# Two chained SCNN layers (five-tap scans down, up, right and left): the last pair's output on two DMA queues with a sixth residual tile, one transfer for the identity, and the second input's statistics on ScalarE

## The chip, the cores and the metric

The kernel runs on one NeuronCore of a Trainium2 chip. The metric is the device time of one execution in microseconds (us). Matrix products run on TensorE (PE in the profile), element-wise work on VectorE (DVE), ScalarE (ACT) and GpSimd (POOL). DMAs are issued from two queues: SyncE's (SP) and ScalarE's (ACTq in a timeline; its transfers are counted as q10, those of SP as q1). A queue issues in order, and an ACT instruction that stands behind an ACT DMA issue waits for it.

## The reference

The input is x of shape (32, 48, 64, 128) in float32: 32 images, 48 channels, 64 rows, 128 columns. Two layers each do x = x + conv(groupnorm(x)), where `conv` is four scans in sequence. Each scan carries one line of the image and adds to the next line a five-tap convolution of it over channels and the other axis:

```python
def step(w, b):
    def f(carry, inp):
        nxt = inp + _conv1d(carry, w, b)      # 48x48 channels, 5 taps
        return (nxt, nxt)
    return f
...
_, d_rest = jax.lax.scan(step(down_w, down_b), d0, xs[1:])      # rows 1..63
...
_, u_rest = jax.lax.scan(step(down_w, down_b), u0, seq)         # rows 62..0, same weights
...
_, r_rest = jax.lax.scan(step(right_w, right_b), r0, ws[1:])    # columns 1..127
...
_, l_rest = jax.lax.scan(step(left_w, left_b), l0, R[Ww - 2::-1])
...
x = x + _L0_conv_ref(_gn(x), ...)
x = x + _L1_conv_ref(_gn(x), ...)
```

`_gn` is a group norm of 16 groups of 3 channels, with mean and variance over a whole image and no learned scale. A scan is serial: 63 steps down, 63 up, 127 right, 127 left.

## The kernel before, in words

**Tiling.** The 32 images are four groups of eight (g = 0 to 3), and two groups make a pair. A scan step is nine matmuls of 128x128 into three PSUM tiles, followed by three VectorE adds (line 660) that add bias and input, and the next step needs their result. A line of an image lies over 128 partitions in three pieces (`NG` = 3): eight interleaved positions (`e`) times 48 channels. The list `PIECES` says which channels of which position lie where, so a load or a store of one piece is three or four DMAs (`pieces(o)`: three for o = 0 and o = 2, four for o = 1).

**Phases.** `PHASES` lists twelve. A "rows" phase does the down and up scan of one group (126 steps), a "cols" phase the right and left scan of one pair (254 steps). The order is rows x0, rows x1, cols pair 0, rows x2, then those of layer 1 mixed in, and last cols (1,0) and cols (1,1). Layer 0's normalised input comes from `xin`, a permuted copy of x in DRAM; results of layer 0 go to `mid`; the up scan's result goes to `upa` or `upb` and is read back by columns.

**Memory.** One big tile, `arena`, holds three slots of 6 units each and four stage units (a unit is 128 partitions x 2048 floats, 1 MB). A pair in a cols phase has four quarters of the width; quarter j lies in slot j % 3, so quarters 0 and 3 share a slot: quarter 0 is written to `spill` after the right scan has passed it and read back (`spill_unit(..., True)`) after quarter 3 has been given out.

**Order.** There is no automatic scheduler. `at(t, fn, ...)` puts a call in an agenda at scan step t (counted over all phases), and each engine's and each queue's instructions are issued in that order. Times in the agenda are steps, of about 2 us each; the real waits come from data. The 8 DMA semaphores (they show as waits of the issuing instruction in the built program) are given out in turn over both queues, so a DMA waits until the one eight before it in program order has landed.

**The start.** `first_group` loads group 0 (`take`, two DMAs per image and half), makes an identity matrix in DRAM (`make_ident`: a block of zeros, then its first column of ones, each one DMA; read back with a row pitch one shorter, the ones fall on the diagonal) and reads it back into `to_row` in ten small DMAs mixed with the loads. The up to three DMAs held back per `let_go` follow between loads.

**The second input.** `plan_input(1, ...)` brings group 1 in during phase 0, in four blocks of 8 + 8 rows, t = 38, 51, 64, 77. Two block buffers (`nats1`) alternate. Of each block POOL makes four permuted tiles of two row pairs (`permute`, line 493, into two ring tiles) and SP writes them to `xin` (`put_out`). Statistics for images 0 to 3 come from VectorE (`stats.take`, line 340), those of 4 to 7 from ScalarE (`take_others`, lines 350 and 358: a pass for the sum and a pass for the squares). The block after next is loaded (`take_in`) at `free`, 12 steps after the block's t, and the fourth permuted tile is written at 12.25 steps. `scaling` then turns statistics into a scale and an offset, one stage per step, `move_rows` loads the rows of phase 1 from `xin`, and `scale_rows` (line 536) scales them on ScalarE before the scan uses them.

**The last pair.** In cols (1,1), each of 24 units (quarter 3 first, then 2, 1, 0) gets its residual (`load_residual`, on the ACT queue) into one of five tiles, an add (line 589: POOL; VectorE for quarter 0), a permute of eight copies over POOL and ACT (line 614; three engines for quarter 0) and its stores (`store_result`, all on SP, 128-byte runs in `out`). Units are planned 4.5 steps apart. The tile of unit u-2 is loaded again for unit u-2+5 after unit u. `last_loads` puts the residual loads of all six units of quarter 0 (20 DMAs) at one time, left + 97, and `last_results` does those six units after the last scan step. In cols (1,0) only quarter 3 is stored directly; the other three quarters are held in DRAM and let out in the next phase.

Of the kernel before, what the change touches and what calls it, by code (L numbers as in the profile page):

```python
# [33 lines left out]
C = 48  # L34
# [7 lines left out]
GB = 8  # L42
# [49 lines left out]
def kernel(  # L92
# [22 lines left out]
    NBN = H * W // (2 * BN)  # L115
    CHANNEL = H * W * GB
    PAD = 1024
    assert N == FULL and SLOT == NG * HALF * N and SLOT == 6 * UNIT

    cpool = ctx.enter_context(tc.tile_pool(name="cpool", bufs=1))  # L120
# [15 lines left out]
    arena = const([FULL, 3 * SLOT + 4 * UNIT], "arena")  # L136
    slot = [arena[:, i * SLOT : (i + 1) * SLOT] for i in range(3)]
    stage = arena[:, 3 * SLOT :].rearrange("p (i n) -> p i n", i=4)
    wt = {k: const([FULL, NG, NG * FULL], f"w{k}") for k in ("right", "left")}
    downs = const([FULL, 2, NG, NG * FULL], "downs")  # L140
    wt |= {f"down{i}": downs[:, i] for i in range(2)}
    spare_tile = downs.rearrange("p i g n -> p (i g n)")[:, 0:UNIT]
    bd = const([FULL, NG, 2, 3], "bd")
    mask_sb = const([P, P], "mask_sb")
    maskp = const([P, NG, FULL], "maskp")
    mask_in = const([FULL, NG, P], "mask_in")
    last = const([FULL, NG * N], "last")
    junk = const([FULL, BN], "junk")

    def kept(name):  # L150

# [470 lines left out]
    def store_result(k, j, i, perm):  # L622
        pair = PHASES[k][2]
        o, half = UNITS[i]
        for e, c0, c1, p0 in pieces(o):
            dst = in_output(j, 2 * pair + half, e)[c0 * NH : c1 * NH]
            src = perm[p0 : p0 + c1 - c0].rearrange("p (a b n) -> p a b n", a=NH, b=GB)
            dma(dst.rearrange("(c a) b n -> c a b n", a=NH), src)

    def hold_result(j, i, perm):  # L630
        o, half = UNITS[i]
# [110 lines left out]

    def plan_input(g, times, work, lag, nats, perms):

        stats = InputStats(f"x{g}", GB // 2 if g == 1 else 0)
        rows = nats[0].shape[-1] // W
        ahead, pieces_of = len(nats), rows * W // BN
        per = rows * W * GB // perms[0].shape[-1]
        for j, t in enumerate(times):
            nat = nats[j % ahead]  # L750
            if j == 0 and g > 1:
                at(t - 7, take_in, g, 0, nat)
            for i in range(per):
                perm, r = perms[i % len(perms)], i * rows // per
                at(t + i * work / per, permute, nat, r, perm, [nc.gpsimd])
                at(t + i * work / per + 4, put_out, g, 2 * rows * j + r, perm, rows)
            for b in range(stats.nv):
                at(t + lag + 1.25 * b, stats.take, pieces_of * j, nat, b)
            at(t + lag, stats.take_others, pieces_of * j, nat)
            if j + ahead < len(times):  # L760
                free = t + max(work, lag + 1.25 * stats.nv, 7)
                at(free, take_in, g, 2 * rows * (j + ahead), nat)
        spread(t + work + lag + (0, 0, 8, 5)[g], scaling(f"x{g}", 0, g, stats, x_masks), 1)

    def plan_rows(k, t0, prev):
        if k == 1:
# [33 lines left out]
    def plan_cols(k, t0, prev):  # L800
        _, layer, pair = PHASES[k]
        n = 2 * NG
        after = prev == "cols"
        for i in range(n):
            if follows(k) and UNITS[i][1] == 1:
                other = nc.scalar
                at(t0 - 31 + i, load_unit, k, 0, i, 4, NH, 0, E8, other)
                at(t0 - 13 + i, load_unit, k, 0, i, 2, 4, 0, E8, other)
                at(t0 - 6 + i / n, load_unit, k, 0, i, 1, 2, 0, E8, other)
                at(t0 - 1.5, load_unit, k, 0, i, 0, 1, E8 // 4, E8, other)  # L810
                at(t0, load_unit, k, 0, i, 0, 1, 0, E8 // 4, other)
            else:
                early = 30 if after else 46 if k == 2 else 70
                at(t0 - early + 2 * i, load_unit, k, 0, i)
            if follows(k):

                at(t0 + 1.5, load_unit, k, 1, i, 0, NH, 0, E8, nc.scalar)
            else:
                at(t0 + (3 if after else -24 + 2 * i), load_unit, k, 1, i)
            at(t0 + (38 if after else 8) + 2 * i, load_unit, k, 2, i)  # L820
            at(t0 + 33 + 2 * i, spill_unit, k, i, False)
            at(t0 + 50 + 2 * i, load_unit, k, 3, i)
        final = k == len(PHASES) - 1
        left = t0 + W - 1
        end = left + W - 1
        for i in range(n):
            at(left + 64 + 2 * i, spill_unit, k, i, True)
        units = []
        for n_done, j in enumerate((3, 2, 1, 0)):
            every = 4.5  # L830
            if j == 0 and PHASES[k + 1 if not final else k][0] == "rows":
                every = 7
            units += [(left + 34 + 32 * n_done + every * i, j, i) for i in range(n)]
        stats = None
        if layer == 0:
            stats = ResultStatsV(f"r{2 * pair}"), ResultStatsA(f"r{2 * pair + 1}")
        tiles = [stage[:, i] for i in range(4)]
        if layer:
            tiles.append(spare_tile)
        n = len(tiles)  # L840
        direct = [u for u in units if not (final and u[1] == 0)]

        for u, (t, j, i) in enumerate(direct):
            nat = tiles[u % n]
            o, half = UNITS[i]
            if u < n:
                at(left + 16, load_residual, k, j, i, nat)
            if layer == 0:
                if u >= n:
                    at(direct[u - n][0] + 3, load_residual, k, j, i, nat)  # L850
                at(t, add_residual, k, j, i, nat)
                at(t + 4, keep_result, k, j, i)
                unit = quarter(k, j)[:, half, o]
                if half == 0:
                    for b in range(GB):
                        at(t + 5 + b, stats[0].take, j, o, unit, b)
                else:
                    at(t + 1, stats[1].take, j, o, unit)
            else:

                at(t, add_residual, k, j, i, nat)
                at(t + 2.5, permute_unit, k, j, i, nat, (nc.gpsimd, nc.scalar, nc.scalar))
                if final or j not in HELD:
                    at(t + 4.5, store_result, k, j, i, nat)
                else:
                    at(t + 4.5, hold_result, j, i, nat)

                if u >= 2 and u - 2 + n < len(direct):
                    at(t + 4.6, load_residual, k, *direct[u - 2 + n][1:], tiles[(u - 2) % n])
        if layer == 0:  # L870
            t = units[-1][0] + 14
            g = 2 * pair
            spread(t, scaling(f"r{g}", 1, g, stats[0], r_masks), 1)
            spread(t + 20, scaling(f"r{g + 1}", 1, g + 1, stats[1], r_masks), 1)
        if layer:

            at(left + 10, nc.scalar.copy, junk[:, 0:1], quarter(k, 3)[:, 0, 0, RUN - 1 : RUN])
        if layer and not final:
            todo = [(j, half, e) for j in HELD for half in range(2) for e in range(E8)]
            for n, what in enumerate(todo):  # L880
                at(end + 63 + 1.9 * n, let_result, *what)
        if final:
            at(left + 97, last_loads, k)
            at(end + 4, last_results, k)

    def last_tiles(k):
# [1 line left out]
        s = slot[slots(k)[2]].rearrange("p (i n) -> p i n", i=2 * NG)  # L888
        return [s[:, i] for i in range(2 * NG)]

    def last_loads(k):
        for i, nat in enumerate(last_tiles(k)):
            load_residual(k, 0, i, nat)

    def last_results(k):

        for i, nat in enumerate(last_tiles(k)):
            perm = (*(stage[:, n] for n in range(4)), spare_tile)[i % 5]
            add_residual(k, 0, i, nat, nc.vector)
            permute_unit(k, 0, i, perm, (nc.scalar, nc.gpsimd, nc.vector))  # L900
            store_result(k, 0, i, perm)
# [10 lines left out]

    tiles = [stage[0:P, i] for i in range(4)]
    nats1 = [wide_nat(2 * SLOT + i * UNIT * 4, 8) for i in range(2)]
    plan_input(1, [starts[0] + 38 + 13 * j for j in range(4)], 11, 7, nats1, tiles[2:4])
    nats = [wide_nat(3 * SLOT, 4)]
    times = [starts[2] + 16 + 13.5 * j for j in range(8)]
    plan_input(2, times, 6, 6, nats, tiles[2:4])
# [13 lines left out]
    def first_group():  # L932
# [10 lines left out]
        spare = {k: wt[k].rearrange("p i n -> p (i n)") for k in ("down1", "right", "left")}  # L943
        to_row = [spare["right"][0:C, i * FULL : (i + 1) * FULL] for i in range(9)]
        to_row += [spare["left"][0:C, 0:FULL]]
        zero, one = last[0:C, 0 : C + 1], last[0:C, C + 1 : C + 2]
        ident = dram.tile([C, C + 1], F32, tag="ident", name="ident")
        square = ident.rearrange("c n -> (c n)")[0 : C * C].rearrange("(c n) -> c n", n=C)

        def make_ident():  # L950
            dma(ident, zero)
            dma(ident[:, 0:1], one)
            for m, (e, c0, c1, o, p0) in zip(to_row, PIECES):
                hold(m[c0:c1, p0 : p0 + c1 - c0], square[c0:c1, c0:c1])

        rows = HALF // 2
        parts = [wide_nat(SLOT + i * 2 * HALF * N * 2, rows) for i in range(2)]
        nc.vector.memset(zero, 0.0)
        nc.vector.memset(one, 1.0)
        for b in range(2 * GB):  # L960
            if b == 2:
                nc.vector.memset(spare["right"], 0.0)
# [37 lines left out]
                    ps.rearrange("p (r n) -> p r n", n=N),  # L1000
                )

        for b in range(3):
            take(0, b)
        make_ident()
        load_weights("down0", 0, DOWN, hold)
        load_constants(hold)
        for b in range(3, GB):
# [123 lines left out]
```

## Time and profile before

| what | us |
|---|---|
| median of 3 runs | 4410.18 (4403.57 to 4413.39) |
| the profiled execution | 4416.53 |
| its span | 4414.7 |
| PE busy | 4154.9 |
| first scan step starts | 149.25 |
| last scan step ends | 4311 |

The span is what the profile covers; 1.8 us lie outside. PE is busy nearly throughout, but that is no measure of a limit: matmuls wait for the previous step's adds. Between the first and the last step PE stands still for some 82 us, 33 of them before 500 us. DMA share is the mean busy share of 16 DMA engines; it goes over 1.00 where transfers of both queues overlap. PEclk is the granted clock.

### The profile page before, as it was taken

The page shows a single profiled execution, that of the slowest core. Times are in us where ns is not written, and L with a number is a line of the kernel's source. Part 1 is how long each engine was busy: PE and PEld are TensorE (multiplying, and loading weights), DVE is VectorE, ACT ScalarE, POOL GpSimd, SP SyncE. Part 2 cuts the span into 40 slices and gives each one's busy share as a digit, 9 for nine tenths or more (in the row PEclk, how much of TensorE's full clock was granted, in tenths as well). Part 3 has the DMA queues.
Part 4 walks back from the last instruction along what each step waited for, and adds up shares of the span by engine and source line. Part 5 has one row for each costly group of instructions (what it writes and reads, how often), then busy time and mean ns, then how long its engine had stood idle before and what let it go on. Part 6 is the DMA issues. An engine that isn't in the chain of part 4 may idle for free.

```text
span 4414.7 us, 89966 instructions
## 1 busy us (share of the span) xinstructions
PE 4154.9 (94%) x36632; PEld 4125.1 (93%) x36632; DVE 2183.1 (49%) x6594; ACT 1311.1 (30%) x2570; POOL 829.0 (19%) x775
## 2 busy tenths in 40 slices
PE   4889998999999999998999999999999999999990
PEld 1889998999999999998999999999999999999990
DVE  5454443446664444443446665444444444444442
ACT  1743301434794545100006764403000011110112
POOL 4342000324332020000004410000000034410443
PEclk9999999999999999999999999999999999999995
DMA  9988879865998989579407989849187059999799
GB/s 180 178 164 152 129 139 186 223 123 186 234 196 147 156 157 160 92 124 207 72 1 238 226 166 139 119 67 163 30 147 169 1 105 229 251 239 162 137 220 148
DMA packets 2111230, 680.34 MB, mean 154 GB/s; under 512 B 2000992, under 2 KB 2053984, under 8 KB 2070880
## 3 DMA queue, kind: packets, MB, share of 16 engines
q1 hardware_dynamic: 2092992, 586.49, 70.0%
q10 hardware_dynamic: 17824, 88.10, 8.4%
q8 instruction: 288, 4.72, 0.5%
q14 instruction: 126, 1.03, 0.1%
HBM read 397.57 MB, written 295.98 MB: 157 GB/s over the span
## 4 chain that ended last, share of the span: by engine, by line
PE 85%; DMA 6%; ACT 4%; SPq 3%; issue 1%; POOL 1%; DVE 0%; ACTq 0%; POOLq 0%; DVEq 0%
PE step_01r L651 6%; PE step_00r L651 6%; PE step_10r L651 6%; PE step_00l L651 6%; PE step_10l L651 6%; PE step_01l L651 6%; PE step_11l L651 5%; PE step_11r L651 4%; PE step_11d L651 3%; PE step_10u L651 3%; PE step_11u L651 3%; PE step_12d L651 3%; PE step_13u L651 3%; PE step_12u L651 3%; PE step_13d L651 3%; PE step_03d L651 3%
## 5 line engine op out<-in xcount | busy, mean ns | idle before, releaser
L536 ACT ACTIVATE arena<-arena,offset,scale 128x256 f32<-128x256 f32 (+2 forms) x864 | 600.9, 790 | 404.0 <-DVE arena L660 214.5
L589 POOL TENSOR_TENSOR arena<-arena 128x2048 f32<-128x2048 f32 x83 | 376.3, 4549 | 1722.3 <-PE step_01l L651 533.4
L493 POOL COPY arena<-arena 112x256 f32<-112x256 f32 x458 | 271.0, 649 | 753.4 <-DMA arena<-in_x 522.7
L427 ACT ACTIVATE junk<-arena 128x256 f32<-128x256 f32 x192 | 129.6, 675 | 693.3 <-DMA arena<-xin 553.2
L651 PE MATMUL step_00r<-arena,wright 128*128 128x128 f32 x2286 | 257.7, 276 | 21.1 <-DMA arena<-upa 21.1
L651 PE MATMUL step_01r<-arena,wright 128*128 128x128 f32 x2286 | 258.0, 277 | 20.8 <-DMA arena<-upa 20.8
L651 PEld LDWEIGHTS step_00r<-arena,wright 128*128 128x128 f32 x2286 | 257.5, 193 | 21.3 <-issue 21.2
L651 PEld LDWEIGHTS step_01r<-arena,wright 128*128 128x128 f32 x2286 | 257.8, 193 | 21.0 <-issue 20.9
L651 PE MATMUL step_11r<-arena,wright 128*128 128x128 f32 x2286 | 258.8, 277 | 5.1 <-DVE arena L660 5.1
L651 PEld LDWEIGHTS step_11r<-arena,wright 128*128 128x128 f32 x2286 | 258.3, 193 | 5.5 <-DVE arena L660 5.3
L651 PE MATMUL step_00l<-arena,wleft 128*128 128x128 f32 x2286 | 256.3, 275 | 0.0
L651 PE MATMUL step_10r<-arena,wright 128*128 128x128 f32 x2286 | 256.1, 275 | 0.0
L651 PEld LDWEIGHTS step_10r<-arena,wright 128*128 128x128 f32 x2286 | 255.8, 192 | 0.3
L651 PEld LDWEIGHTS step_00l<-arena,wleft 128*128 128x128 f32 x2286 | 255.7, 192 | 0.0
L651 PE MATMUL step_11l<-arena,wleft 128*128 128x128 f32 x2286 | 255.5, 275 | 0.0
L651 PE MATMUL step_10l<-arena,wleft 128*128 128x128 f32 x2286 | 255.5, 275 | 0.0
L651 PE MATMUL step_01l<-arena,wleft 128*128 128x128 f32 x2286 | 255.4, 275 | 0.0
L651 PEld LDWEIGHTS step_11l<-arena,wleft 128*128 128x128 f32 x2286 | 255.4, 192 | 0.0
L651 PEld LDWEIGHTS step_10l<-arena,wleft 128*128 128x128 f32 x2286 | 255.4, 192 | 0.0
L651 PEld LDWEIGHTS step_01l<-arena,wleft 128*128 128x128 f32 x2286 | 255.3, 192 | 0.0
L614 ACT COPY arena<-arena 128x256 f32<-128x256 f32 x190 | 109.6, 655 | 474.4 <-POOL arena L589 246.9
L358 ACT ACTIVATE junk<-arena 112x512 f32<-112x512 f32 x160 | 101.0, 631 | 501.3 <-DMA arena<-in_x 253.9
(177 smaller groups left out, 7025.9 us busy)
## 6 DMA issues: line engine op xcount, KB each, us to landing
xin<-arena SPq DMA_DIRECT2D x96, 384.0 KB, 5.4
arena<-xin SPq DMA_DIRECT2D x96, 384.0 KB, 8.2
mid<-arena SPq DMA_DIRECT2D x96, 384.0 KB, 7.8
arena<-mid SPq DMA_DIRECT2D x192, 192.0 KB, 4.3
upb<-arena SPq DMA_DIRECT2D x192, 192.0 KB, 3.9
arena<-upb SPq DMA_DIRECT2D x96, 384.0 KB, 11.4
arena<-xin SPq DMA_DIRECT2D x186, 192.0 KB, 4.3
upa<-arena SPq DMA_DIRECT2D x180, 192.0 KB, 3.9
```

What stands on the lines that cost most here:

```text
L358: nc.scalar.activation(junk[0:P], piece, AF.Identity, accum_out=self.sum[:, at[0], at[1]],)
L427: nc.scalar.activation(junk[:, 0:n], view[:, b], AF.Identity, accum_out=self.sum[:, i, j : j + 1])
L493: copy(dst[:, r, q], src[:, r0 + r, q])
L536: nc.scalar.activation(args[0], args[0], AF.Identity, bias=args[2], scale=args[1])
L589: eng.tensor_tensor(unit, unit, nat, ALU.add)
L614: copy(by_w(perm)[:, a], src[:, a])
L651: nc.tensor.matmul(part(whole(ps[o]), -s), weights[:, i, FULL * (o - NG * s - i + 1) : FULL * (o - NG * s - i + 2)], part(src(i), s), star ...
```

## The change

- Identity: the block of zeros and the ones are set together in SBUF and written to DRAM in one DMA, after the first image's loads and not after the third's.
- Second input: all eight images' statistics go to ScalarE, from step t + 2 (before t + 7); a block buffer is loaded again at t + 13.5 for g = 1 (before t + 12), which lies behind the write of the fourth permuted tile; `scaling` starts at step 93 (before 95).
- Layer 1's two cols phases: `spill` is read back a unit at a time from left + 39.5, 4.5 steps apart, each behind the unit's stores (before: from left + 64, 2 apart).
- Last pair: every second store goes to the ACT queue; a sixth residual tile; the residual of a unit of quarter 0 is loaded behind the same unit of quarter 1 and `last_loads` is gone; quarter 0's six permuted units have six tiles (before five).
- To make room, two weights, `last` and `junk` lie with `down0` and `down1` in one tile, `early`, of which two units are used as residual tiles at the end.

```diff
-    downs = const([FULL, 2, NG, NG * FULL], "downs")
-    spare_tile = downs.rearrange("p i g n -> p (i g n)")[:, 0:UNIT]
+    early = const([FULL, 3 * WEIGHTS + NG * N + BN], "early")
+    spare_tiles = [early[:, i * UNIT : (i + 1) * UNIT] for i in range(2)]
...
     def store_result(k, j, i, perm):
-        for e, c0, c1, p0 in pieces(o):
+        for n, (e, c0, c1, p0) in enumerate(pieces(o)):
...
-            dma(dst.rearrange("(c a) b n -> c a b n", a=NH), src)
+            queue = nc.scalar if n % 2 and k == len(PHASES) - 1 else nc.sync
+            dma(dst.rearrange("(c a) b n -> c a b n", a=NH), src, queue)
...
-        stats = InputStats(f"x{g}", GB // 2 if g == 1 else 0)
+        stats = InputStats(f"x{g}", 0)
...
-            for b in range(stats.nv):
-                at(t + lag + 1.25 * b, stats.take, pieces_of * j, nat, b)
             at(t + lag, stats.take_others, pieces_of * j, nat)
             if j + ahead < len(times):
-                free = t + max(work, lag + 1.25 * stats.nv, 7)
+                free = t + (13.5 if g == 1 else 7)
                 at(free, take_in, g, 2 * rows * (j + ahead), nat)
-        spread(t + work + lag + (0, 0, 8, 5)[g], scaling(f"x{g}", 0, g, stats, x_masks), 1)
+        spread(t + work + lag + (0, 3, 8, 5)[g], scaling(f"x{g}", 0, g, stats, x_masks), 1)
...
-            at(left + 64 + 2 * i, spill_unit, k, i, True)
+            t = left + 64 + 2 * i if layer == 0 else left + 39.5 + 4.5 * i
+            at(t, spill_unit, k, i, True)
...
-            tiles.append(spare_tile)
+            tiles += spare_tiles[0 : 2 if final else 1]
...
+                if final and j == 1:
+                    at(t + 4.7, load_residual, k, 0, i, last_tiles(k)[i])
...
-            at(left + 97, last_loads, k)
...
-            perm = (*(stage[:, n] for n in range(4)), spare_tile)[i % 5]
+            perm = (*(stage[:, n] for n in range(4)), *spare_tiles)[i]
...
-    plan_input(1, [starts[0] + 38 + 13 * j for j in range(4)], 11, 7, nats1, tiles[2:4])
+    plan_input(1, [starts[0] + 38 + 13 * j for j in range(4)], 11, 2, nats1, tiles[2:4])
...
         def make_ident():
-            dma(ident, zero)
-            dma(ident[:, 0:1], one)
+            dma(ident, one)
...
-        nc.vector.memset(zero, 0.0)
-        nc.vector.memset(one, 1.0)
+        nc.vector.memset(one, 0.0)
+        nc.vector.memset(one[:, 0:1], 1.0)
...
-        for b in range(3):
+        take(0, 0)
+        make_ident()
+        for b in range(1, 3):
             take(0, b)
-        make_ident()
```

More of the change, by code (lines that the diff above doesn't have):

```diff
@@ L117 @@
     PAD = 1024
+    WEIGHTS = NG * NG * FULL
     assert N == FULL and SLOT == NG * HALF * N and SLOT == 6 * UNIT
@@ L138 @@
     stage = arena[:, 3 * SLOT :].rearrange("p (i n) -> p i n", i=4)
-    wt = {k: const([FULL, NG, NG * FULL], f"w{k}") for k in ("right", "left")}
-    downs = const([FULL, 2, NG, NG * FULL], "downs")
-    wt |= {f"down{i}": downs[:, i] for i in range(2)}
-    spare_tile = downs.rearrange("p i g n -> p (i g n)")[:, 0:UNIT]
+    early = const([FULL, 3 * WEIGHTS + NG * N + BN], "early")
+    spare_tiles = [early[:, i * UNIT : (i + 1) * UNIT] for i in range(2)]
+    wt = {
+        k: early[:, i * WEIGHTS : (i + 1) * WEIGHTS].rearrange("p (i n) -> p i n", i=NG)
+        for i, k in enumerate(("down0", "down1", "right"))
+    }
+    wt["left"] = const([FULL, NG, NG * FULL], "wleft")
     bd = const([FULL, NG, 2, 3], "bd")
@@ L146 @@
     mask_in = const([FULL, NG, P], "mask_in")
-    last = const([FULL, NG * N], "last")
-    junk = const([FULL, BN], "junk")
+    last = early[:, 3 * WEIGHTS : 3 * WEIGHTS + NG * N]
+    junk = early[:, 3 * WEIGHTS + NG * N :]
     def kept(name):
@@ L875, in plan_cols @@
         if layer:
-            at(left + 10, nc.scalar.copy, junk[:, 0:1], quarter(k, 3)[:, 0, 0, RUN - 1 : RUN])
+            at(left + 10, nc.scalar.copy, junk[:, BN - 1 :], quarter(k, 3)[:, 0, 0, RUN - 1 : RUN])
         if layer and not final:
@@ L889, in last_tiles @@
         return [s[:, i] for i in range(2 * NG)]
-    def last_loads(k):
-        for i, nat in enumerate(last_tiles(k)):
-            load_residual(k, 0, i, nat)
     def last_results(k):
         for i, nat in enumerate(last_tiles(k)):
-            perm = (*(stage[:, n] for n in range(4)), spare_tile)[i % 5]
+            perm = (*(stage[:, n] for n in range(4)), *spare_tiles)[i]
             add_residual(k, 0, i, nat, nc.vector)
@@ L945, in first_group @@
         to_row += [spare["left"][0:C, 0:FULL]]
-        zero, one = last[0:C, 0 : C + 1], last[0:C, C + 1 : C + 2]
+        one = last[0:C, 0 : C + 1]
         ident = dram.tile([C, C + 1], F32, tag="ident", name="ident")
```

## The prediction

> **What bounds the kernel now.** First the page's busy time, then the stages, then the timelines of the queues where PE stands still. The scan is a serial chain of 4161 us, from the first step at 149.25 to the last at 4311. Nothing in the change touches a step, so it can act in three places: the 149 us ahead of the chain, the chain's own gaps (82 us), and the 104 us behind it.
>
> ```profile
> span 4414.7 us, 89966 instructions
> PE 4154.9 (94%) x36632; PEld 4125.1 (93%) x36632; DVE 2183.1 (49%) x6594; ACT 1311.1 (30%) x2570; POOL 829.0 (19%) x775
> ```
>
> The stages (columns: stretch, its length, busy time of PE, PEld, DVE, ACT, POOL, clock, DMA share, GB/s) show a hole in the DMA at the start, and in the end stage a full DMA with holes:
>
> ```profile
> 18.00:24.00 6.00, 0.00 (x0) 0.00 (x0) 5.59 (x8) 0.00 (x0) 0.00 (x0) 1.00 0.33 71
> 24.00:60.00 36.00, 17.29 (x19) 6.01 (x20) 21.30 (x35) 6.93 (x11) 4.74 (x8) 1.00 1.03 184
> ...
> 4106.00:4130.00 24.00, 24.00 (x217) 24.00 (x217) 11.53 (x36) 2.89 (x5) 9.99 (x5) 1.00 0.05 9
> 4198.00:4298.00 100.00, 100.00 (x897) 100.00 (x897) 47.63 (x149) 11.69 (x21) 43.37 (x28) 1.00 1.07 228
> 4298.00:4314.00 16.00, 13.02 (x117) 12.83 (x115) 8.92 (x22) 6.30 (x11) 0.00 (x0) 1.00 0.87 159
> 4338.00:4350.00 12.00, 0.00 (x0) 0.00 (x0) 0.00 (x0) 2.77 (x5) 1.75 (x3) 0.50 0.71 119
> 4386.00:4402.00 16.00, 0.00 (x0) 0.00 (x0) 0.00 (x0) 0.00 (x0) 0.00 (x0) 0.50 0.73 122
> ```
>
> **Identity.** SP stands still for the two writes:
>
> ```profile
> 5.33 13.72 SPq L193 DMA_DIRECT2D ident<-last  x2
> ```
>
> The first write is queued behind six loads of 384 KB and lands 13.4 us later; nothing else is issued meanwhile, and when the loads are through (18 us) the DMA runs dry. With two loads ahead of it (0.8 MB at 170 GB/s, 4.6 us) the one write lands near 10 us, while four loads are still moving, and SP goes on. What is won is the hole, not SP's 13.7 us: (1.0 - 0.33) x 6 = 4 us, and a little of the ramp after it, say 5. Since the DMA share is 0.95 from 60 to 149 us, the loads set the first step's time, and the 5 us move it. Bounds: 0 (other waits set it) to 9 us (SP's whole lead). I take 5.
>
> **Second input.** The up scan of phase 0 stands still from 298.7 to 312.3 because VectorE's statistics wait in its queue for the fourth block:
>
> ```profile
> 257.30 13.83 SPq L193 DMA_DIRECT2D arena<-in_x  x16
> 272.24 20.27 SPq L193 DMA_DIRECT2D xin<-arena  x8
> 297.60 12.31 SPq L193 DMA_DIRECT2D arena<-in_x  x16
> ...
> 282.21 9.45 POOL L493 COPY arena<-arena 112x256 f32<-112x256 f32 x16 [19.12 <-DMA xin<-arena]
> 321.78 9.45 POOL L493 COPY arena<-arena 112x256 f32<-112x256 f32 x16 [19.12 <-DMA xin<-arena]
> ...
> 310.74 1.29 DVE L340 BATCH_NORM_STATS2 bn_x<-arena 112x6 f32<-112x512 f32 x2 [11.73 <-DMA arena<-in_x]
> ```
>
> Taking the 64 VectorE instructions away (0.68 us each, 44 us) does not win the 13 us by itself: phase 1 can't run before its rows are in `xin`, read back and scaled. That chain is the one to follow. POOL's permutes wait twice for 19.1 us, since the write of a block's fourth tile stands on SP behind the sixteen loads of the next block, so its ring tile isn't free. The new `free` puts that write ahead of the loads. With the row's own durations (a tile 4.73 us on POOL, sixteen loads 13.8 us on SP, a write landing 4 us after issue, 9 behind loads): block 0's fourth write lands at 262 and not 281; block 1's tiles end at 263, 268, 286, 291 (before: 302.7); block 3's loads go out at 292 (297.6); block 2's tiles end at 296, 300, 320, 324; block 3's at 329, 334, 339, 343. POOL was through at 358.3. So SP comes to the 20 row loads of phase 1 at 344 in place of 359.3: 15 us earlier. From there SP is issue-bound by a full DMA (100 row DMAs from 359 to 483, share 1.03 between 400 and 500), so rows 32 to 47, which phase 1 waited for until 482.3, come 15 us earlier too.
>
> Is ScalarE in time? Its instructions are 0.76 us apart in the first pass, 0.85 in the second. A block now has 16 of each: 25.8 us and not 12.9. From 225.5, where ScalarE came to them, four blocks end at 251, 277, 303 and 329, provided that their loads are there (before: 328.75, with waits of 51 us between). Queued behind them on ACT is the standard deviation and then the scaling of phase 1's rows, which waited for loads until 378.7. VectorE reaches the variance at step 96. Without the old stall that is step 84 (298) plus 12 x 2.02 = 322, so the stall doesn't vanish: about 7 us of it come back as a wait for ScalarE. The up scan then ends at 329 + 30 x 2.02 + 2 (slower clock after a stop: 0.86 granted from 300 to 350) = 391 rather than 400. Phase 1's first rows are scaled by 385, its rows 16 to 31 by 428 (wanted at 424), rows 32 to 47 by 467 against 482. I take 15 us. Bounds: 0 (another wait on SP or ACT restores the old time) to 20.
>
> Later phases follow: their agenda is counted in steps, the DMA share from 500 to 600 us is 0.66, and the two gaps of 21 us at the starts of cols phases are a fixed store and reload.
>
> **Spill, layer 1.** Six 1 MB loads each, with the same wait as the stores that they now follow; they only move. In cols (1,0) they leave a fuller stretch for one at share 0.53 to 0.83 (3550 to 3700), whose backlog ends in a stop of 5.8 us at 3921. I take 2 us, bounds -3 to 8 (the stop and the slow clock after it).
>
> **End stage.** The queue that goes wrong is ACT:
>
> ```profile
> 4264.52 36.71 ACTq L193 DMA_DIRECT2D arena<-mid  x20
> 4301.27 0.65 ACT L614 COPY arena<-arena 128x256 f32<-128x256 f32 x1 [45.01 <-PE step_11l L651]
> ...
> 4315.76 4.50 POOL L589 TENSOR_TENSOR arena<-arena 128x2048 f32<-128x2048 f32 x1 [39.05 <-DMA arena<-mid]
> ```
>
> The twenty residual loads for quarter 0, needed only after 4311, hold ACT for 37 us, and behind them stand the copies and the last residuals of quarter 1. So SP's stores starve, and after 4338 only stores are left. One at a time they give less. Per queue (packets, MB, share), first 4242 to 4266, then 4354 to 4386:
>
> ```profile
> q1 hardware_dynamic: 19118, 2.43, 72.2%
> q10 hardware_dynamic: 421, 2.43, 38.3%
> ...
> q1 hardware_dynamic: 37077, 4.72, 92.5%
> ```
>
> Mixed with loads the engines do 204 to 228 GB/s at a share of 1.07, stores alone 147 to 155 at 0.93. The work from 4106 on stays the same: 25.2 MB of stores, 20 of loads, 6.3 of spill. The change recovers idle DMA. The sixth tile puts 1 MB into the empty 4106 to 4130: 5 us. The holes at 4186 to 4198 (share 0.76), 4298 to 4314, 4338 to 4350 and 4386 to 4402 are worth 3 + 3 + 3 + 3.5 us, smaller ones 2.5. About 5 MB of stores move out of the stores-only end (33 us at 0.93) into the mix (1.07): 4 us. Together 24 us; quarter 0's own 6.3 MB can't start before 4311, and 24 us less leaves 80, twice what these need (6.3 / 155 = 41 us). I take three quarters, 18 us, for new waits. Bounds: -10 to 35.
>
> Does the second queue itself make stores faster? By the mixed row, 6.3 MB at 208 GB/s would be 30 us and not 41. The Trainium skill (Trainium Kernel Development and Optimization, Key Constraints) says that DMAs of SP and ACT run on the same 16 engines and that issuing from several "only saves the sequencer's issue time". No row shows 128-byte stores on both queues; the mixed row owes its rate to 8 KB pieces. By the rule the gain is 0, by the row 11 us. I take 0 and keep 11 in the upper bound.
>
> **Sum.** 5 + 15 + 2 + 18 = 40 us: the execution's span goes from 4414.7 to 4375. It took 4416.53 and lies 6 us above the median of 4410.2; the same 40 us off the median give **4370 us**.
>
> **Rivals.**
> - *The stall only changes hands.* ScalarE's fourth block comes late (each load of it that arrives after 303 pushes the 329), or SP's order still holds POOL: phase 1 starts its rows 32 to 47 at 482 again. For it: VectorE gets 7 us of wait back even in my own sum. Against it: 51 us of waits on ScalarE to absorb. Left: 5 + 2 + 18, so 4385.
> - *The end stage is bound by the DMA and regains nothing but the tile's 5 us.* For it: share 1.07 for 100 us. Against it: 4298 to 4402. Left: 5 + 15 + 2 + 3, 4385 to 4390. With both rivals 4400 to 4405.
> - *Slower: ACT becomes the end stage's bound.* 24 units have 32 of their 80 stores on ACT, ahead of the next unit's copies. Over the 285 us from 4130 ACT has about 70 us of copies (24 x 2.9) and 65 of residual issues. SP's store issues took 2.9 us in the median, up to 14.9. At 2.9 ACT is held 93 us, 228 in all, and fits. From 4.7 us it is full and the gain is gone; 22 us are won elsewhere, so from 4.7 + (18 + 22) / 32 = 6 us per store the kernel is slower. At 6.5 us: 4425. The two queues share the engines, which speaks for longer issues; [...]SP's get shorter, which speaks against.
>
> **How the numbers follow.** All parts: 0.55, range 4350 to 4390. First rival 0.15, second 0.15, both 0.05, slower 0.10. About 0.2% (9 us) is what a measurement tells from no change: faster means under 4401. Both-rivals is the case within; of the single ones a tenth falls there too. Faster 0.83, same 0.07, slower 0.10. The low end adds the better bounds (two-queue stores, 20 us in front): 4410 - 65 = 4345. The high end takes in the singles and half of both: 4402; outside are the slower case and some 5 in 100 below.
>
> **What would show it.** The first step at 144; `ident` one write landing near 10 us; no POOL wait of 19 us before 330 and row loads of phase 1 issued near 339 (344 less 5); a VectorE wait of some 7 us for ScalarE near step 96; phase 1's last stop ending near 462. In the end stage no ACTq group of twenty loads, quarter 1's adds on POOL finished near 4311's counterpart, DMA share above 0.9 to the end, and 86 us rather than 104 behind the last step. It is wrong if ACT's store issues run above 5 us, if loads of block 3 arrive after 310, or if phase 1 waits for rows 32 to 47 as long as before.

## The result, and the profile after

The changed kernel takes **4375.17 us** (median of 6 runs, 4370.57 to 4386.64), against 4410.54 us for the kernel before in the same series: a ratio of 0.9927, 95% interval 0.991 to 0.9944, that is 25 to 40 us. The forecast was 4370 us, with a range of 4345 to 4402. The profiled execution took 4375.56 us.

The busy times hardly move and say little, as before:

```profile
span 4373.8 us, 90099 instructions
PE 4149.4 (95%) x36632; PEld 4120.7 (94%) x36632; DVE 2164.2 (49%) x6558; ACT 1360.7 (31%) x2698; POOL 820.4 (19%) x775
```

A better ledger is where each scan begins and ends. The queries by tile give the first and last start of a scan's matmuls (in each line after the min/median/max of one matmul in ns). First the kernel before, for the first scan, the down scan of phase 1 and the last scan:

```profile
L651 PE MATMUL step_00d<-arena,downs x1134: 268/275/582, 104.2 to 255.3; 128*128 128x128 f32 x189
L651 PE MATMUL step_01d<-arena,downs x1134: 267/275/582, 400.2 to 547.6; 128*128 128x128 f32 x189
L651 PE MATMUL step_11l<-arena,wleft x2286: 262/275/307, 4055.6 to 4310.7; 128*128 128x128 f32 x191
```

Then the same three after the change:

```profile
L658 PE MATMUL step_00d<-arena,early x1134: 268/275/583, 94.8 to 244.4; 128*128 128x128 f32 x189
L658 PE MATMUL step_01d<-arena,early x1134: 267/275/582, 395.3 to 533.9; 128*128 128x128 f32 x189
L658 PE MATMUL step_11l<-arena,wleft x2286: 262/275/307, 4038.5 to 4293.7; 128*128 128x128 f32 x191
```

Two readings follow. The first: the first step of the kernel before is at 104.2 and not at 149.25, where the table ahead of the prediction and its first paragraph put it. 149.25 is where a stop of 10 us ends; the scan had begun 45 us earlier. So the chain is 4206 us long and not 4161, and PE stands still in it for 93 us and not 82. The second: of the 40.9 us between the two spans, 37.6 come from three of these four stretches.

| stretch | before | after | difference |
|---|---|---|---|
| start to first step | 104.2 | 94.8 | -9.4 |
| first step to the end of phase 1's down scan | 443.4 | 439.1 | -4.3 |
| from there to the last step | 3763.1 | 3759.8 | -3.3 |
| last step to the end | 104.0 | 80.1 | -23.9 |

Each is one execution. How far such a stretch wanders by itself is seen from the experiments below; the third, 3.3 us, is within it.

**The start.** SP issues the one write behind two loads and waits 3.9 us for it, not 13.7:

```profile
3.47 0.42 SPq L199 DMA_DIRECT2D ident<-early  x1
3.94 1.81 SPq L199 DMA_DIRECT2D arena<-in_x  x4
9.68 1.24 SPq L199 DMA_DIRECT2D early<-ident  x3
```

The stages (same columns as before) show the hole from 18 to 24 us closed, and the stretch after it, which had a share of 1.03 before at 184 GB/s, moving 216 at a share of 1.01. The four stretches of the end stage that follow are those shown for the kernel before, 17 us earlier; the last line is the stretch in which only stores are left:

```profile
18.00:24.00 6.00, 0.00 (x0) 0.00 (x0) 5.59 (x8) 0.00 (x0) 0.00 (x0) 1.00 1.02 202
24.00:60.00 36.00, 24.44 (x27) 8.48 (x28) 25.87 (x43) 7.83 (x13) 7.62 (x14) 1.00 1.01 216
4089.00:4113.00 24.00, 24.00 (x217) 24.00 (x217) 11.45 (x36) 2.90 (x5) 10.08 (x5) 1.00 0.24 50
4181.00:4281.00 100.00, 100.00 (x897) 100.00 (x897) 47.53 (x149) 20.24 (x35) 56.03 (x36) 1.00 1.22 189
4281.00:4297.00 16.00, 12.94 (x116) 12.74 (x115) 9.21 (x23) 4.64 (x9) 6.70 (x5) 1.00 1.21 211
4321.00:4333.00 12.00, 0.00 (x0) 0.00 (x0) 3.85 (x3) 3.47 (x6) 2.12 (x3) 0.50 1.27 204
4337.00:4361.00 24.00, 0.00 (x0) 0.00 (x0) 2.02 (x3) 6.93 (x12) 2.12 (x3) 0.50 1.40 166
```

**The second input.** In the timelines POOL still waits for its ring tiles, 16 us in place of 19, and VectorE stops twice, now for ScalarE (SP, then POOL, then VectorE):

```profile
252.54 13.69 SPq L199 DMA_DIRECT2D arena<-in_x  x16
288.16 15.03 SPq L199 DMA_DIRECT2D arena<-in_x  x16
...
277.79 9.43 POOL L499 COPY arena<-arena 112x256 f32<-112x256 f32 x16 [15.97 <-DMA xin<-arena]
314.50 9.32 POOL L499 COPY arena<-arena 112x256 f32<-112x256 f32 x16 [16.35 <-DMA xin<-arena]
...
316.13 0.22 DVE L382 TENSOR_REDUCE mean_x_x<-sum_x_x 112x8 f32<-112x64 f32 x1 [8.73 <-ACT early L364]
329.93 0.55 DVE L387 TENSOR_TENSOR neg_x_x<-neg_x_x,mean_x_x 112x64 f32<-112x64 f32 x1 [11.70 <-ACT early L356]
```

So a stop of 11.7 us became two of 20.4 together; of the 10.9 us by which the up scan begins earlier (244.5 against 255.4), 4.3 are left at its end (395.2 against 399.5).

**The end stage.** ACT has no group of twenty loads any more, and quarter 1's last add is through 2.6 us before the last step. In the kernel before (third line) it began 23 us behind it:

```profile
4278.47 2.99 ACTq L199 DMA_DIRECT2D arena<-mid  x3
...
4286.58 4.53 POOL L595 TENSOR_TENSOR arena<-arena,early 128x2048 f32<-128x2048 f32 x1 [8.07 <-DMA early<-mid]
...
4333.41 4.50 POOL L589 TENSOR_TENSOR arena<-arena 128x2048 f32<-128x2048 f32 x1 [4.38 <-ACT arena L614]
```

From 4337 to 4361 only stores are moving, on both queues (packets, MB, share):

```profile
q10 hardware_dynamic: 15931, 2.03, 70.3%
q1 hardware_dynamic: 15438, 1.96, 69.4%
```

That is 4.0 MB in 24 us, 166 GB/s, where one queue gave 147 at a share of 0.925. The next lines are the whole stretch behind the last step, before and after (without a microsecond at the end), and then the 168 us up to 13 us ahead of it, again before and after:

```profile
4311.00:4414.00 103.00, 0.02 (x1) 0.00 (x0) 23.87 (x19) 21.64 (x38) 39.79 (x30) 0.52 0.91 147
4294.00:4373.00 79.00, 0.00 (x0) 0.00 (x0) 24.01 (x19) 18.90 (x33) 12.74 (x18) 0.52 1.26 174
...
4130.00:4298.00 168.00, 168.00 (x1506) 168.00 (x1506) 80.11 (x250) 31.87 (x55) 84.95 (x56) 1.00 1.02 204
4113.00:4281.00 168.00, 168.00 (x1507) 168.00 (x1506) 80.10 (x250) 37.63 (x65) 97.59 (x64) 1.00 1.22 202
```

Behind the last step there were 15.2 MB at 147 GB/s before and 13.8 MB at 174 GB/s after. The 1.4 MB that were gone by then are worth 1.4 / 147 = 9 us, the better rate 13.8 / 147 - 13.8 / 174 = 15 us. The sixth tile is seen in the first hole (4089 to 4113): 9 GB/s became 50, which is 1 MB in 24 us. In the 168 us of the last two lines the DMA moved no more than before. What changed there is the mix: a part of quarter 0's residual loads now lies behind the last step, and stores took their place ahead of it. Behind the last step are now about 9.7 MB of stores and 4.2 of loads, before 12.7 and 2.6 (by the counts of packets of 128 bytes and of 8 KB).

### The profile page after: what moved, and what is told of

It reads as the page before. It is cut to its first block, busy times and chain, and to the rows that moved or that the text cites. A ratio compares the mean times of both kernels' runs of the same rounds, so it can differ in the third digit from the quotient of the medians.

```text
span 4373.8 us, 90099 instructions
## 1 busy us (share of the span) xinstructions
PE 4149.4 (95%) x36632; PEld 4120.7 (94%) x36632; DVE 2164.2 (49%) x6558; ACT 1360.7 (31%) x2698; POOL 820.4 (19%) x775
## 5 line engine op out<-in xcount | busy, mean ns | idle before, releaser
L433 ACT ACTIVATE early<-arena 128x256 f32<-128x256 f32 x192 | 129.5, 675 | 687.5 <-DMA arena<-xin 547.4
L658 PE MATMUL step_00r<-arena,early 128*128 128x128 f32 x2286 | 258.6, 277 | 22.6 <-DMA arena<-upa 22.6
L658 PEld LDWEIGHTS step_00r<-arena,early 128*128 128x128 f32 x2286 | 258.4, 194 | 22.9 <-issue 22.8
L658 PE MATMUL step_01r<-arena,early 128*128 128x128 f32 x2286 | 257.4, 276 | 20.1 <-DMA arena<-upa 20.1
L658 PEld LDWEIGHTS step_01r<-arena,early 128*128 128x128 f32 x2286 | 257.1, 193 | 20.4 <-issue 20.3
L364 ACT ACTIVATE early<-arena 112x512 f32<-112x512 f32 x192 | 121.0, 630 | 460.5 <-PE step_00r L658 246.6
L658 PE MATMUL step_11r<-arena,early 128*128 128x128 f32 x2286 | 258.9, 277 | 3.9 <-DVE arena L667 3.9
L658 PEld LDWEIGHTS step_11r<-arena,early 128*128 128x128 f32 x2286 | 258.2, 193 | 4.4 <-DVE arena L667 4.2
L658 PE MATMUL step_10r<-arena,early 128*128 128x128 f32 x2286 | 256.0, 275 | 0.0
L658 PEld LDWEIGHTS step_10r<-arena,early 128*128 128x128 f32 x2286 | 255.7, 192 | 0.3
L658 PE MATMUL step_01l<-arena,wleft 128*128 128x128 f32 x2286 | 255.4, 275 | 0.0
L658 PEld LDWEIGHTS step_10l<-arena,wleft 128*128 128x128 f32 x2286 | 255.4, 192 | 0.0
L658 PEld LDWEIGHTS step_11l<-arena,wleft 128*128 128x128 f32 x2286 | 255.4, 192 | 0.0
```

The costliest lines, as they stand in the source:

```text
L364: nc.scalar.activation(junk[0:P], piece, AF.Identity, accum_out=self.sum[:, at[0], at[1]],)
L433: nc.scalar.activation(junk[:, 0:n], view[:, b], AF.Identity, accum_out=self.sum[:, i, j : j + 1])
L658: nc.tensor.matmul(part(whole(ps[o]), -s), weights[:, i, FULL * (o - NG * s - i + 1) : FULL * (o - NG * s - i + 2)], part(src(i), s), star ...
```

## Experiments

Theory: three parts that add up, each worth what the ledger says (9, 4, 24). Rivals: the sizes of the forecast (5, 15, 18), and parts that swallow each other. The four kernels and the kernel before ran in one series, in which the kernel before took 4414.57 us (26 runs).

**The identity alone.**

```diff
-            dma(ident, zero)
-            dma(ident[:, 0:1], one)
+            dma(ident, one)
...
-        for b in range(3):
+        take(0, 0)
+        make_ident()
+        for b in range(1, 3):
             take(0, b)
-        make_ident()
```

> The kernel before with the identity's change alone. Theory A (what is won at the start is carried to the end, since phase 1 waits for a chain of loads that begins with the first ones): the first scan step starts near 95 us instead of 104.2, every later phase starts 8 to 11 us earlier, and the time falls by 9 us to 4401. Theory B (as forecast: only the hole in the DMA counts): 5 us. Theory C (the stop of the up scan swallows it): the up scan ends within 2 us of 399.5 and the time doesn't fall by more than 2.

Measured: 4405.96 us, ratio 0.9984 (0.9975 to 0.9993), 7 us less (3 to 11). In its trace the scans begin and end as follows:

```profile
L651 PE MATMUL step_00d<-arena,downs x1134: 268/275/582, 96.8 to 250.0; 128*128 128x128 f32 x189
L651 PE MATMUL step_01d<-arena,downs x1134: 268/275/582, 394.8 to 540.4; 128*128 128x128 f32 x189
```

The first step comes 7.4 us earlier than in the kernel before, the up scan and phase 1 begin 5 us earlier (8 to 11 were expected), phase 1's down scan ends 7.2 us and the last step 10.3 us earlier. The three other executions of this series with the old identity have their first step at 103.5, 107.1 and 106.6; with 104.2 that is 105.4 in the mean, against 95.8 for the two with the new one: 9.6 us. The start's lead is carried to the end, so C falls. A and B differ by 4 us, which the interval doesn't part; the first steps speak for A, since all four with the old identity lie at 103 us or later and both with the new one below 97.

**The second input alone**, in the kernel before: statistics on ScalarE from t + 2, `scaling` from step 93, the buffer loaded again at 13.5 steps.

```diff
-        stats = InputStats(f"x{g}", GB // 2 if g == 1 else 0)
+        stats = InputStats(f"x{g}", 0)
...
-            for b in range(stats.nv):
-                at(t + lag + 1.25 * b, stats.take, pieces_of * j, nat, b)
...
-                free = t + max(work, lag + 1.25 * stats.nv, 7)
+                free = t + (13.5 if g == 1 else 7)
...
-        spread(t + work + lag + (0, 0, 8, 5)[g], scaling(f"x{g}", 0, g, stats, x_masks), 1)
+        spread(t + work + lag + (0, 3, 8, 5)[g], scaling(f"x{g}", 0, g, stats, x_masks), 1)
...
-    plan_input(1, [starts[0] + 38 + 13 * j for j in range(4)], 11, 7, nats1, tiles[2:4])
+    plan_input(1, [starts[0] + 38 + 13 * j for j in range(4)], 11, 2, nats1, tiles[2:4])
```

> The kernel before with the second input's change alone: all statistics on ScalarE, buffer loaded again at 13.5 steps. Theory A (the two phases' starts in the trace of the changed kernel: of 13.7 us of lead at the end of phase 1, 9.4 were there at the first step): 4 us, 4406; VectorE waits 9 + 12 us for ScalarE and the up scan ends later than before by some 5 us. Theory B (as forecast): 15 us, 4395, from POOL's shorter waits.

Measured: 4408.55 us, ratio 0.9988 (0.9979 to 0.9996), 5 us less (2 to 9). B's 15 us are out. The profiled execution is the slowest of the eleven (its span is that of the kernel before), so its lines serve for the order and the waits and not for the gain. Those that decide are SP's row loads for phase 1, the two stops of VectorE, PE's last stop in phase 1 with VectorE's wait for the rows that makes it, and phase 1's down scan:

```profile
357.13 20.84 SPq L193 DMA_DIRECT2D arena<-xin  x20
...
326.60 0.22 DVE L376 TENSOR_REDUCE mean_x_x<-sum_x_x 112x8 f32<-112x64 f32 x1 [10.45 <-ACT junk L358]
340.41 0.66 DVE L381 TENSOR_TENSOR neg_x_x<-neg_x_x,mean_x_x 112x64 f32<-112x64 f32 x1 [11.51 <-ACT junk L350]
...
478.47 21.71 PE L651 MATMUL step_01d<-arena,downs 128*128 128x128 f32 x167 [7.23 <-DVE arena L660]
478.07 0.35 DVE L660 SCALAR_TENSOR_TENSOR arena<-step_01d,bd,arena 128x128 f32<-128x128 f32 x1 [8.44 <-DMA arena<-xin]
...
L651 PE MATMUL step_01d<-arena,downs x1134: 268/275/582, 406.8 to 543.6; 128*128 128x128 f32 x189
```

The row loads and the last stop in the kernel before:

```profile
359.26 22.84 SPq L193 DMA_DIRECT2D arena<-xin  x20
...
482.31 17.90 PE L651 MATMUL step_01d<-arena,downs 128*128 128x128 f32 x131 [4.83 <-DVE arena L660]
```

The row loads go out at 357.1 and not at 344 (359.3 before), and rows 32 to 47 are there at 478.5 (482.3 before). The up scan ends at 406.7, 7 us *later* than before, and still phase 1's down scan ends at 543.6, 4 us earlier: what phase 1 waits for last is its rows, and the stops of the up scan lie in their shade.

**The order on SP alone**: only `free` is changed, the statistics stay half on VectorE.

```diff
-                free = t + max(work, lag + 1.25 * stats.nv, 7)
+                free = t + (13.5 if g == 1 else 7)
```

> The kernel before with the buffer loaded again at 13.5 steps in place of 12, statistics still half on VectorE. If the order on SP is what wins time and the statistics' move costs it: POOL's two waits fall from 19 us as in the changed kernel (16), VectorE's stop of 11.7 us gets shorter by the 5 us that the fourth block comes earlier, the up scan ends some 5 us earlier, and the time falls by 4 to 6 us, as much as or more than with the statistics moved too. If the move of the statistics is what wins: no change within 3 us.

Measured: 4409.17 us, ratio 0.9986 (0.9978 to 0.9995), 6 us less (2 to 10), as much as with the statistics moved too.

```profile
358.44 22.81 SPq L193 DMA_DIRECT2D arena<-xin  x20
...
278.92 1.29 DVE L340 BATCH_NORM_STATS2 bn_x<-arena 112x6 f32<-112x512 f32 x2 [3.12 <-DMA arena<-in_x]
315.67 1.29 DVE L340 BATCH_NORM_STATS2 bn_x<-arena 112x6 f32<-112x512 f32 x2 [8.48 <-DMA arena<-in_x]
...
480.68 19.54 PE L651 MATMUL step_01d<-arena,downs 128*128 128x128 f32 x152 [5.96 <-DVE arena L660]
...
L651 PE MATMUL step_01d<-arena,downs x1134: 268/275/582, 404.3 to 545.3; 128*128 128x128 f32 x189
```

Its first step came at 107.1, so from the first step its row loads are at 251.3, against 253.6 in the second input's kernel and 255.1 in the kernel before. VectorE's stop for the fourth block falls to 8.5 us, but it now stops 3.1 us for the third as well, 11.6 together and no less than before. So the up scan, which was expected to end 5 us earlier, ends 2 us later counted from the first step (297.1 against 295.3), and still phase 1's down scan is through 5 us earlier. As far as the intervals tell, the gain is there without moving a single statistic; they would still hide a few microseconds either way. From the first step to the end of phase 1's down scan the kernels need 443.4 (before), 443.6 (identity), 440.1 (second input), 438.2 (this one) and, with the same front as before, 447.3 in the next: such a stretch wanders by 4 us, so what settles the sizes here is the intervals, and they hold 2 to 10 us for both.

**The end stage alone**: the changed kernel with the identity and the second input (its start times too) as before; what is left is the end stage, the spill and the shared tile.

```diff
-            dma(ident, one)
+            dma(ident, zero)
+            dma(ident[:, 0:1], one)
...
-        stats = InputStats(f"x{g}", 0)
+        stats = InputStats(f"x{g}", GB // 2 if g == 1 else 0)
...
-                free = t + (13.5 if g == 1 else 7)
+                free = t + max(work, lag + 1.25 * stats.nv, 7)
...
```

> The changed kernel with the identity and the second input as before: what is left is the end stage and the spill. Theory A (24 us between the last scan step and the end are its own): 80 us behind the last step in place of 104, the scan up to there within 3 us of before, and the time falls by 24 to 27 us, to about 4385. Theory B (part of the 24 us comes from the earlier start): less than 18.

Measured: 4394.18 us, ratio 0.9951 (0.9937 to 0.9964), 22 us less (16 to 28).

```profile
L658 PE MATMUL step_11l<-arena,wleft x2286: 262/275/307, 4061.4 to 4316.6; 128*128 128x128 f32 x191
...
4317.00:4398.00 81.00, 0.00 (x0) 0.00 (x0) 23.27 (x19) 18.90 (x33) 17.82 (x20) 0.52 1.28 176
```

The span is 4398.7, so 82.1 us lie behind the last step, against 104.0 in the kernel before and 80.1 in the changed one, and they run at 176 GB/s. That is theory A in the trace: the end stage's gain is its own. The 22 us measured lie just under A's 24 to 27; the interval holds A and doesn't exclude B's bound of 18. The last step is at 4316.6, 6 us later than in the kernel before's execution, where within 3 us was expected; 2.4 are there at the first step and 6.3 at the end of phase 1's down scan. Nothing in this kernel's front differs from that of the kernel before except the place of some tiles. The profiled execution is the slowest of the five, 6 us above their median, so I take the delay for scatter, without having shown it.

The gains of the three parts, 7 + 5 + 22, make 34 us, against the 32 (25 to 40) of all together. With the intervals of both sides they add up to within some 10 us; that the parts swallow more of each other than that falls.

**What stays open.** The four edits of the end stage (second queue, loads of quarter 0 unit by unit, sixth tile, earlier spill) were not undone one at a time. That ACT's group of twenty loads is gone, that the stores-only stretch is faster and that less is left at the last step is seen in the traces; how the 22 us divide over the edits is not. Nor was a kernel run in which phase 1's row loads are put ahead of the up scan's stores on SP, which the finding about the rows suggests.

## Why the prediction was right, and where it was not

The time, the sign and the range were right, and the sum of the four terms, 40 us, stands beside 41 in the profiled pair and 32 (25 to 40) in the timed ratio. The terms are less good than their sum: 2 and 4 us too little at the two ends, 10 and 2 too much between them. That these nearly cancel is luck.

- **Identity, 5 us forecast, 7 (3 to 11) measured, 9.6 in the first steps.** Mis-sized. I counted the hole in the DMA share and held that from 24 us on a share of 1.03 means full. It doesn't: the same stretch then moved 216 GB/s at 1.01. That the loads up to 149 us set the first step was wrong as well, since it was at 104.2. SP's lead, 10.4 us at the first `ident` read (20.1 against 9.7), was the upper bound that I gave (as 9), and nearly all of it came through.
- **Second input, 15 forecast, 5 (2 to 9) measured.** This term failed, at the step "POOL was through at 358.3" to "343". The mechanism is there (the fourth write ahead of the loads, SP 2 us earlier with its row loads), but in the kernel with this part alone POOL ends at 354.1:

```profile
259.77 14.89 SPq L193 DMA_DIRECT2D arena<-in_x  x16
296.51 16.96 SPq L193 DMA_DIRECT2D arena<-in_x  x16
...
286.09 9.47 POOL L493 COPY arena<-arena 112x256 f32<-112x256 f32 x16 [16.37 <-DMA xin<-arena]
323.42 9.35 POOL L493 COPY arena<-arena 112x256 f32<-112x256 f32 x16 [16.41 <-DMA xin<-arena]
344.74 9.38 POOL L493 COPY arena<-arena 112x256 f32<-112x256 f32 x16 [1.44 <-DMA xin<-arena]
```

  The sum took 13.8 us for each group of sixteen loads and 9 for a write behind them. The loads took 14.9 and 17.0, the writes 10.5 and 8.9 (275.6 to 286.1, 314.5 to 323.4), which makes 6 of the 11 us. The rest is gaps of about a microsecond between groups and tiles, which the sum left out. Both terms come twice in the chain, since two pairs of tiles wait for writes that now stand behind the *next* sixteen loads: 16 of POOL's 19 us stay. And of POOL's 4 us only 2 are left at SP's row loads (357.1 against 359.3).
- **"About 7 us come back as a wait for ScalarE."** It was 20 us in the changed kernel, 22 with this part alone. The second pass on ScalarE ends at 340 there and not at 329. Its passes over the fourth block take 25.9 us, as in the sum, but begin at 314.5 and not at 303, after a wait of 11 us for a load: that block's loads go out from 296.5 to 313.5. And I had only asked when the variance is wanted, not the sum, two steps earlier. As far as the runs tell, this error cost nothing: the rows, not the up scan, bind phase 1. So the first rival (the stall only changes hands) took place in large part, and by the second of its two reasons, SP's order that still holds POOL: rows 32 to 47 came 4 us earlier and not 15.
- **Spill, 2 forecast: not seen.** From the end of phase 1's down scan to the last step the two kernels with the new spill need 3759.8 and 3762.7 us, the four without it 3763.1, 3760.0, 3765.8 and 3759.3. The stop in the last right scan is 3.9 and 5.9 us with it, 3.9 to 5.5 without.
- **End stage, 18 forecast, 22 (16 to 28) measured, 22 to 24 in the traces.** The reading of ACT's twenty loads held, and the full count of the holes, 24 us, was the better value than three quarters of it; the second rival, 5 us for the tile alone, falls. Where they were won is not as counted: by bytes the holes between 4130 and 4298 gave nothing (204 and 202 GB/s), the tile's 1 MB and 13 us at 212 GB/s in place of 159 just ahead of the last step gave 9 us, and the rate behind it 15, for which the forecast had 6.5 in holes and 4 in a better mix.
- **The second queue, 0 to 11 us, 0 taken.** The Trainium skill's rule (Trainium Kernel Development and Optimization, Key Constraints: several issuing engines only save issue time) and the stores' rows differ a little: 147 GB/s on one queue with its issue gaps, 162 in the best 8 us found (4372 to 4380, before), 166 on both. The quarter's 6.3 MB take 43, 39 and 38 us at these, so 5 us go against the mean and 1 us against the best stretch. The last may still be issue time; no run has the end stage with all stores on SP. The mixed row's 208 GB/s, from which the 11 us came, were not reached by stores alone on both queues.
- **The slower rival.** ACT as the bound would have needed 6 us per store on its queue. The median is 0.6 us and the longest 5.1, while SP's smaller share of them took 1.4 and 2.8 us in the median by tile (2.9 and 2.3 before, all on SP). ACT had room.
- **The signs.** The single `ident` write, POOL's waits below 19 us, ACT without its twenty loads and quarter 1's adds came as said; the stop that ended at 149.25 ends at 140.0 (144 was said), and 80 us are left behind the last step (86). Not as said: the row loads at 346.0 (339), VectorE's wait of 20 us (7), and phase 1's last stop, which ends at 468.6 (462). Of the signs of being wrong one came: the fourth block's last loads, issued at 303, land some 9 us later (the median of the sixteen is 8.6), so after 310.
- **The range.** Its low end takes off 65 us; the bounds that it names make no more than 60 (40 + 11, and 5 to 9 in front).

## What to carry to other kernels

When a queue moves ahead, ask what the next consumer really waits for, and follow that chain with each transfer at the length that it has behind other transfers, not at its median. A stop on a busy engine that lies in the shade of a later transfer can double (here from 12 to 22 us) without showing in the time, and work moved off that engine then wins nothing that the runs can tell: the order on SP alone gave 6 us (2 to 10), with the move of 64 statistics it was 5 (2 to 9). At the end of a kernel, look first for loads that are issued in one block long before they are needed ahead of work that is needed at once.

## What was not expected of the hardware

The share of the DMA engines was no measure of full: with both queues storing 128-byte pieces it reached 1.40 at 166 GB/s, 0.925 with one queue at 147, and at the start 1.03 went with 184 GB/s and 1.01 with 216. Nor does a share over 1.00 need both queues: from 24 to 60 us in the kernel before, nearly all of it was SP's.

```profile
q1 hardware_dynamic: 2419, 6.61, 102.7%
```

A store of the last pair was issued from ACT in 0.6 us in the median, also where SP's took 1.4 and 2.8 (from the changed kernel):

```profile
L199 SPq DMA_DIRECT2D out<-arena x32: 590/1438/8292, 4110.4 to 4353.8; - x32
L199 ACTq DMA_DIRECT2D out<-arena x24: 597/632/5052, 4110.4 to 4348.4; - x24
```
